# A graph network on one core: layer 0 sums its first 208 edge tiles by counting, and table biases come from TensorE

## Chip, cores and metric

The kernel runs on one core of a Trainium2 chip. The metric is the device time of one execution in microseconds. In the text, PE is TensorE, DVE is VectorE, ACT is ScalarE, POOL is GpSimd and SP is SyncE; PEld is the loading of weights into PE, PEclk the share of its clock that PE was granted, and SPq is the queue from which SP issues transfers.

## The reference

There are 3125 nodes with 128 features, x, and 100,000 edges from `src` to `dst`, sorted by `dst`. Each edge has 16 attributes and one of four types. Two layers follow each other, each with a residual and a layer norm. Cut to what matters:

```python
msgs   = x[src]                                     # layer 0
summed = segment_sum(msgs, dst, n_nodes)
deg    = segment_sum(ones, dst, n_nodes)
h      = layernorm(x + elu((summed / max(deg, 1)) @ W + b))

xl = einsum('nf,rfh->nrh', h, W_l) + b_l            # layer 1, r is one of 4 types
xr = einsum('nf,rfh->nrh', h, W_r) + b_r
z  = leaky_relu(xl[src, type] + xr[dst, type] + edge_features)
# attention of 4 heads: a softmax of z . att over the edges of one node and type,
# weighted sums of xl[src, type], means and gates over types, layer norm, a small MLP, layer norm
```

Layer 0 is a mean over incoming edges of a row of x, a product with W, and a norm. Layer 1 needs, for every node and type, a row of two tables, `xl` and `xr`, with 512 columns each.

## The kernel before

The edges are cut into 784 tiles of 128 (`TT`), in order of `dst`, and four tiles are a quad (`NQ` = 196 quads). The main path is the function `windows`. A second path, `general`, runs afterwards and overwrites the output if a check of the data (the row `bad`, summed into `flag`) says that the quads span more nodes than the main path allows.

**Preparation.** `src`, `dst` and the types are loaded by rows, transposed on PE into columns (`src_e`, `loc_e`, `typ_e`: one column per tile, one partition per edge), and turned into masks. `loc_e` is an edge's node relative to its tile's window. `tmr` is a one-hot over the four types.

**Layer 0's loop.** It has one step per quad. A gather (`gather`) is an indirect transfer issued by POOL: it fetches 128 rows of x by the indices in `src_e` into `xg`, which has 24 buffers. In a step,

- `onehot4` makes on DVE, for each of the four tiles, a one-hot of the edges' local node (`oh`, 32 wide); `sums0` multiplies on PE `oh` by the gathered rows (`sg`, four products of 129 columns, the last column being ones for the degree), and after each product issues the gather of the tile 24 further on. ACT copies the result to `sgs`;
- `spread0` makes on DVE a second one-hot (`ohq`), `out0` multiplies by it on PE (`fo`), and `add0` adds `fo` on DVE into `acc0`, at a column that is read from `d0_i` into a register;
- `masked`, `turned` and `keep` prepare layer 1's edge features: DVE multiplies the quad's attributes by the type's one-hot (`em`), PE transposes (`mp`), ACT copies (`emt`), and SP stores to `eam_d`. The attributes come in seven chunks of 112 rows (`load_chunk`; the last has 109 whole rows), which `turn_chunk` transposes into `ee` (`erows` has one buffer).

**Blocks.** A block is 128 nodes, 25 of them (`NB2`). When the sorted edges have passed a block's nodes (`behind`), `block` puts its work into the following steps: `take`, `mean`, `stats`, `scaled`, `turn` end layer 0 for the block, `lin` makes 16 extra columns, and `table(r)`, one type per step, makes the rows of both tables: on PE the products with `wl` and `wr` (`xp`), on DVE the additions of the bias tables `cl` and `cb`, both held for all 128 partitions (into `xlr` and `xf`), on ACT a rounded copy `xh`. `half(r)` subtracts that on DVE and stores both halves to `xr_d`; a last job stores `xlr` to `xl_d` for all four types at once.

**Order.** The object `Ordered` (its `issue` is L647, so most instructions carry that line) makes each engine issue in program order. `at_step(s, engine, f)` puts a job into a step; the loop at the end of the layer runs the jobs of a step around the fixed parts:

```python
if s < NQ:
    turned(s)
if 0 < s <= NQ:
    keep(s - 1); out0(s - 1)
if s + 1 < NQ:
    onehot4(s + 1); masked(s + 1)
...                                   # jobs for DVE and ACT
if s < NQ:
    spread0(s)
if 0 < s <= NQ:
    add0(s - 1)
if s < NQ:
    sums0(s)
```

Weights for the biases are prepared in the first steps (`linear_weights`, `constant`), and `rows_of_sources` turns `src_e` into indices of `xl_d` (`xli_e`) and the type mask into `tng`.

**Layer 1** begins when the pools of layer 0 are released and its tables are stored. It has again one step per quad: POOL gathers rows of `xl_d`, SP loads windows of `xr_d` (`win`) and the stored attributes (`ea`), PE sums them up in `z`, and so on. After it follow a norm, a small MLP and the output.

Of the kernel before, what the change touches and what calls it, by code (L numbers as in the profile page):

```python
# [624 lines left out]
TC = TT // TR  # L625
GT = 8
# [35 lines left out]

def windows_of(u):
    k = 4 if u < UQ else 2 if u < UP else 1
    return [(i, k) for i in range(0, 4, k)]
# [15 lines left out]
def windows(ctx: ExitStack, tc: tile.TileContext, a, out, flag):  # L681
# [13 lines left out]
    xli_e = S["xli_e"] = cst.tile([P, TT], I32, name="xli_e")  # L695
# [10 lines left out]
    tng = cst.tile([P, TT, R], BF16, name="tng")  # L706
# [35 lines left out]
    with tc.tile_pool(name="l0c", bufs=1) as l0c:  # L742
        acc0 = l0c.tile([P, 2, NPW], F32, name="acc0")
        src_e = l0c.tile([P, TT], I32, name="src_e")

        XG = 24
        xg = l0c.tile([P, XG, F + 1], F32, name="xg")
        nc.vector.memset(xg[:, :, F:], 1.0)
        pool = Ordered(tc, nc.gpsimd)
# [5 lines left out]
        with tc.tile_pool(name="pr", bufs=1) as pr, tc.tile_pool(name="prp", bufs=2, space=PSUM) as prp:  # L755
# [26 lines left out]

            srci = rows("srci", "src", 0, nc.scalar)
# [7 lines left out]
            bad = pr.tile([P, 8], F32, name="bad")  # L791
# [3 lines left out]
            nc.vector.memset(acc0, 0.0)  # L795

            src = floats("src", srci)
            to_e(src_e, src)
            for t in range(XG):
                gather(t)  # L800
# [25 lines left out]
            rF, rL, rB = (rfl[:, i] for i in range(3))  # L826
            wt = prp.tile([TR, TC], F32, name="fp_")
# [9 lines left out]
            nc.vector.tensor_copy(d0_i, rB[0:1])  # L837
            typ = floats("typ", typi)
            to_e(typ_e, typ)
            tm = l0c.tile([P, TT, R], BF16, name="tmr")  # L840
# [29 lines left out]
            rF4, rL4 = (x[0:1].rearrange("p (u i) -> p u i", i=4) for x in (rF, rL))  # L870
            for j, (w, x, y) in enumerate((
# [4 lines left out]
                count(1 + j, n)  # L876

# [7 lines left out]
            bp = prp.tile([1, 8], F32, name="bp", bufs=1)  # L885
# [18 lines left out]
        with tc.tile_pool(name="m0c", bufs=1) as m0c, tc.tile_pool(name="l0", bufs=2) as l0, \  # L904
# [4 lines left out]
            one = l0e.tile([1, 1], F32, name="one")  # L909
            nc.vector.memset(one, 1.0)  # L910
# [12 lines left out]
            fb = l0e.tile([P, TT], F32, name="fb")  # L923
# [4 lines left out]
            cl = m0c.tile([P, R, XW], F32, name="cl")  # L928
            cb = m0c.tile([P, R, HC], F32, name="cb")
# [11 lines left out]
            def load_table_weights():  # L941
# [4 lines left out]
                sp.dma_start(cl[:, :, :HC], bass.AP(tensor=a["L1_gnn_b_l"].tensor, offset=a["L1_gnn_b_l"].offset,  # L946
                                                    ap=[[0, P], [HC, R], [1, HC]]))
# [30 lines left out]
            def rows_of_sources():  # L978

                ve.tensor_scalar_min(xli_e, typ_e, float(R - 1))  # L980
                ve.scalar_tensor_tensor(xli_e, src_e, R, xli_e, op0=OP.mult, op1=OP.add)
                ve.tensor_scalar(tng, tm, 1.0, BIG, op0=OP.subtract, op1=OP.mult)

            def linear_weights(r, w):
                def f():

                    at_ = m0.tile([P, HC], F32, name="xf")
                    sp.dma_start(at_, bcast(a["L1_gnn_att"][r], HC, P))
                    tmp = m0.tile([P, HC], F32, name="tmp", bufs=1)
                    ve.tensor_mul(tmp, w[:, r, :HC], at_)  # L990
                    ve.tensor_reduce(w[:, r, HC:XW], tmp.rearrange("p (h c) -> p h c", h=H), AX.X, OP.add)
                    ve.tensor_scalar(w[:, r, HC:XW], w[:, r, HC:XW], SLOPE, None, op0=OP.mult)
                return f

            def constant(r):
                def f():
# [3 lines left out]
                    cp = bank().rearrange("p a b -> p (a b)")  # L1000
                    pe.matmul(cp, cr[:, r:r + 1].to_broadcast([DR + 1, P]), cw, start=True, stop=True)
                    act.activation(cb[:, r], cp, AF.Copy)
# [3 lines left out]
            for i, f in enumerate([edge_weights, rows_of_sources] +  # L1006
                                  [linear_weights(r, w) for r in range(R) for w in (wl, cl)] +
                                  [constant(r) for r in range(R)]):
                at_step(4 + i, "ve", f)
# [4 lines left out]
            def load_chunk(c):  # L1014
                rows = erows[c] = l0e.tile([TR, P * DE], F32, name="earow")
                v = a["edge_attr_16"].rearrange("e d -> (e d)")
                w = P * DE
                o = c * TR * w
# [667 lines left out]
```

## Time and profile before

| | |
|---|---|
| median of three runs | 3029.38 us (3024.73 to 3030.09) |
| profiled execution, its own time | 3014.4 us |
| its span, first to last instruction | 3012.6 us |
| busy over the span: PE, DVE, ACT, POOL | 84%, 60%, 29%, 52% |
| first gather of x | 20.3 us |
| layer 0's loop, first `sg` product | 64 us |
| last `sgs` copy of layer 0 | 1157.8 us |
| last write of `xh` | 1225.3 us |
| first gather of `xl` (layer 1) | 1234.6 us |
| granted PE clock, mean | 0.851 |

How to read it: the span is the profiled execution; everything in it is in microseconds from its start. The 40 slices of the page are 75.3 us each, and a digit is the busy share of a slice in tenths. A line of an answer on busy time by stage gives the stage, its length, then for each engine the busy time and the number of instructions, the granted PE clock, the share of the transfer engines and GB/s. A line of the timeline gives the start, the duration, the engine, the line of the source, the operation, output and inputs, and in brackets the idle time of the engine before it with what ended it. A line of the waits gives who waited for whom, in total, how often, and the longest.

### The profile page before, as it was taken

To read this page: it belongs to the slowest core of one execution; us is meant where nothing else is said; L and a number is where in the kernel's file an instruction comes from. 1 tells how busy PE (TensorE), PEld (TensorE's weight loads), DVE (VectorE), ACT (ScalarE), POOL (GpSimd) and SP (SyncE) were. 2 spreads that over 40 slices of the span, in tenths; PEclk is the share of its full clock that TensorE was granted. 3 is DMA by queue.
4 is the path that set the end of the run, shared out by engine and by line. 5 is a ranking of instruction groups with operands and counts; after the bars stand their busy time and mean duration, and the time that the engine had idled before them with its cause. 6 is when DMAs were issued, how large, how long until landed. Compare 5 with 4: busy or idle time off the path is not lost.

```text
span 3012.6 us, 69650 instructions
## 1 busy us (share of the span) xinstructions
PE 2521.1 (84%) x25681; PEld 1858.9 (62%) x25681; DVE 1794.3 (60%) x6092; ACT 867.3 (29%) x1872; POOL 1552.6 (52%) x1578
## 2 busy tenths in 40 slices
PE   2867777767567777699999999999999999999952
PEld 1444444434244343477777777888888888788832
DVE  6523445455455565367666667667666666566667
ACT  1212223233233232233333333333333333233211
POOL 5777777777756650444444444444444444444200
PEclk9555667677767687899999999999999999999956
DMA  5433545465445554777777777888888899999710
GB/s 154 141 111 98 162 140 184 162 202 186 154 172 191 174 185 169 271 225 221 221 227 221 222 224 231 256 257 255 255 258 252 255 260 259 245 253 258 189 34 23
DMA packets 278166, 599.24 MB, mean 199 GB/s; under 512 B 47142, under 2 KB 98647, under 8 KB 273820
## 3 DMA queue, kind: packets, MB, share of 16 engines
q1 hardware_dynamic: 186568, 334.42, 34.2%
q0 software_dynamic: 87808, 258.61, 30.5%
q8 instruction: 206, 3.38, 0.5%
q10 hardware_dynamic: 3440, 1.66, 0.3%
q14 instruction: 144, 1.17, 0.1%
HBM read 460.02 MB, written 134.48 MB: 197 GB/s over the span
## 4 chain that ended last, share of the span: by engine, by line
PE 50%; DMA 6%; DVE 3%; issue 0%; SPq 0%; ACT 0%; DVEq 0%; ACTq 0%
PE z L647 30%; PE row L647 9%; PE ag L647 6%; DMA win<-xr_d 4%; PE fo L647 2%; PE sm_p L647 2%; DMA ea<-eam_d 1%; DMA out_dram<-o 0%; DMA fh_all<-fh_d 0%; DMA rm<-rm_d 0%; PE hm L1640 0%; DVE fst L1599 0%; PE xp L647 0%; DMA xr_d<-xh 0%; SPq L647 0%
## 5 line engine op out<-in xcount | busy, mean ns | idle before, releaser
L647 POOL DMA_INDIRECT xl<-xl_d,xli_e x784 | 754.0, 962 | 958.3 <-DVE r L647 326.1
L647 POOL DMA_INDIRECT xg<-in_x_dram,src_e x784 | 797.4, 1017 | 323.0 <-issue 132.0
L647 ACT ACTIVATE relu<-z 128x512 f32<-128x512 f32 x784 | 468.4, 597 | 1104.5 <-PE z L647 1102.7
L647 PE MATMUL z<-f_ident,xl 128*128 128x128 f32 x3136 | 475.6, 274 | 0.0
L647 PEld LDWEIGHTS z<-f_ident,xl 128*128 128x128 f32 x3136 | 368.5, 141 | 44.5 <-issue 0.6
L647 PE MATMUL z<-ea,weh 128*128 128x512 f32 x784 | 383.9, 490 | 12.6 <-DMA sg<-seg_d 12.6
L647 PE MATMUL z<-oht,win 96*128 96x128 f32 (+2 forms) x1600 | 346.9, 298 | 16.5 <-DMA win<-xr_d 16.2
L647 PEld LDWEIGHTS z<-oht,win 128*128 128x128 f32 (+1 forms) x1600 | 276.8, 190 | 77.0 <-DMA win<-xr_d 10.3
L647 PE MATMUL z<-ea,wel 128*128 128x512 f32 x784 | 311.3, 397 | 0.0
L647 PE MATMUL fo<-ohq,sgs 128*128 128x64 f32 x784 | 168.3, 357 | 164.2 <-ACT sgs L647 68.5
L647 PE MATMUL sg<-xg,oh 128*32 128x129 f32 x1568 | 200.6, 361 | 122.8 <-DMA xg<-in_x_dram,src_e 120.7
L647 PEld LDWEIGHTS fo<-ohq,sgs 128*128 128x128 f32 x784 | 153.7, 274 | 193.0 <-ACT sgs L647 130.7
L647 PE MATMUL row<-relu,attw 128*32 128x128 f32 x6272 | 248.5, 276 | 0.0
L647 PEld LDWEIGHTS sg<-xg,oh 128*32 128x32 f32 x1568 | 64.5, 126 | 281.6 <-DMA xg<-in_x_dram,src_e 184.3
L647 DVE TENSOR_TENSOR oh<-loc_e,iw 128x128 f32<-128x128 bf16 (+1 forms) x294 | 99.1, 337 | 217.1 <-PE sg L647 216.7
L647 PE MATMUL ag<-xl,wo 128*32 128x128 f32 x6272 | 218.8, 280 | 3.4 <-DVE wo L647 3.4
L647 PEld LDWEIGHTS z<-ea,weh 128*128 128x128 f32 x784 | 148.1, 189 | 89.6 <-issue 89.5
L647 PE MATMUL mp<-f_ident,em 128*128 128x128 f32 x784 | 178.8, 369 | 11.0 <-issue 5.1
L647 ACT ACTIVATE xh<-xf 128x512 fp32r<-128x512 f32 x100 | 63.0, 630 | 431.5 <-DVE xf L647 257.1
L647 PEld LDWEIGHTS row<-relu,attw 128*32 128x32 f32 x6272 | 164.0, 110 | 32.7 <-issue 32.7
L647 PEld LDWEIGHTS ag<-xl,wo 128*32 128x32 f32 x6272 | 164.4, 112 | 7.2 <-DVE wo L647 3.7
L647 DVE TENSOR_TENSOR acc<-acc,fo 128x128 f32 (+1 forms) x392 | 99.5, 254 | 115.0 <-issue 44.1
(270 smaller groups left out, 3602.4 us busy)
## 6 DMA issues: line engine op xcount, KB each, us to landing
win<-xr_d SPq DMA_DIRECT2D x224, 256.0 KB
xr_d<-xh SPq DMA_DIRECT2D x100, 512.0 KB
eam_d<-emt SPq DMA_DIRECT2D x196, 256.0 KB
ea<-eam_d SPq DMA_DIRECT2D x196, 256.0 KB
win<-xr_d SPq DMA_DIRECT2D x176, 192.0 KB
xl_d<-xlr SPq DMA_DIRECT2D x25, 1032.0 KB
sg<-seg_d SPq DMA_DIRECT2D x196, 128.0 KB
rm<-rm_d SPq DMA_DIRECT2D x392, 32.1 KB
```

The lines of the kernel that those rows point to most:

```text
L647: ins = f(*args, **kw)
```

## The change

**Counting.** The first 52 quads (`UD`; 208 tiles, `TD`), whose nodes are below 240 (`ND`), no longer gather. For a tile, DVE makes two one-hots in bf16: `ol`, 128 wide, of the source node's low seven bits, and `oc`, 200 or 300 wide, of its upper bits times 8 or 12 plus the local destination. PE multiplies them (`cn`, in a PSUM tile called `dn`), summed over the quad's four tiles: how often each source occurs at each destination. `count_add` adds this on DVE to `A`, 128 x 25 x 252. At the end `counted_sums` multiplies on PE, for each of 25 source blocks, the block of x and a matrix of ones by `A` (240 columns), and one addition puts the sums and degrees into `acc0`.

**The loop** has 144 steps (`NS`), from quad 52 on. 52 counts are spread over its first 39 steps or so, counted sums over the following 13. `turned_by` spreads all 196 quads of edge attributes over 140 steps. Edge attributes come in 14 chunks of 56 rows, the last with 53 whole rows. Blocks 0 and 1 come after the counted sums, the others 52 steps earlier than before. The jobs of a step stand in another order, with the copy `sgs` first on ACT.

**Biases.** `cl` and `cb` go. One small tile, `cbl` (four partitions, in fp32r, the biases as high and low halves), is multiplied by two rows of ones (`two`) on PE, ahead of each table product into the same PSUM tile. ACT copies the sums out (`xh`, `xlr`), DVE only makes the low half. `xl_d` is stored one type at a time, two steps after its table.

**Buffers.** `src_e` and `tm` are overwritten in place by what was `xli_e` and `tng`, in `rows_of_sources`, which moves from the start to step `NS`. `fb` lies in `wl` until that is loaded. `xh` and `xlr` have three buffers, `xp` three instead of four, `em` four, `oh` three. Three checks are added to `bad`.

The diff, cut to its core:

```diff
+UD, ND, SHI = 52, 240, NB2
+def counted(u):
+    return 8 if u < 24 else 12
...
-            for t in range(XG):
+            for t in range(TD, TD + XG):
                 gather(t)
...
+            nc.vector.tensor_scalar_min(dc_i, rF4[:, :UD, 0], float(ND - 1))
...
+            for u0, u1, j in ((0, 24, 8), (24, UD, 9)):
+                nc.vector.scalar_tensor_tensor(sj[:, :u1 - u0], rF4[:, u0:u1, 0], float(counted(u0) - 1),
+                                               rL4[:, u0:u1, 3], op0=OP.add, op1=OP.is_lt)
+                count(j, u1 - u0)
+            nc.vector.tensor_scalar(bad[0:1, 10:11], rL[0:1, TD - 1:TD], float(ND - 1), None, op0=OP.is_gt)
...
-            cl = m0c.tile([P, R, XW], F32, name="cl")
-            cb = m0c.tile([P, R, HC], F32, name="cb")
+            cbl = m0c.tile([4, R, XW], F32R, name="cbl")
+            two = m0c.tile([4, 2, P], F32R, name="two")
...
             def rows_of_sources():
-                ve.tensor_scalar_min(xli_e, typ_e, float(R - 1))
-                ve.scalar_tensor_tensor(xli_e, src_e, R, xli_e, op0=OP.mult, op1=OP.add)
                 ve.tensor_scalar(tng, tm, 1.0, BIG, op0=OP.subtract, op1=OP.mult)
+                ve.tensor_scalar_min(typ_e, typ_e, float(R - 1))
+                ve.scalar_tensor_tensor(src_e, src_e, R, typ_e, op0=OP.mult, op1=OP.add)
+            def halves(r, p0, row):
+                n = row.shape[-1]
+                hi = m0.tile([1, 2, XW], F32R, name="xh", bufs=3)
+                act.activation(hi[:, 0, :n], row, AF.Copy)
+                ve.tensor_sub(hi[:, 1, :n], row, hi[:, 0, :n].bitcast(F32))
+                for i in range(2):
+                    sp.dma_start(cbl[p0 + i:p0 + i + 1, r, :n].bitcast(F32), hi[:, i, :n].bitcast(F32))
...
+            def turned_by(s):
+                return min(NQ, (s + 1) * NQ // (NS - 4) + 1)
...
+            def count_columns():
+                ve.memset(A, 0.0)
+                ve.tensor_scalar(tmp_i, src_e[:, :TD], P - 1, None, op0=OP.bitwise_and)
+                ve.tensor_copy(lo_f, tmp_i)
+                ve.tensor_scalar(tmp_i, src_e[:, :TD], 7, None, op0=OP.logical_shift_right)
+                ve.tensor_copy(c_f, tmp_i)
+                for u0, u1 in ((0, 24), (24, UD)):
+                    c = c_f[:, 4 * u0:4 * u1]
+                    ve.tensor_scalar(c, c, float(counted(u0)), -200.0, op0=OP.mult, op1=OP.add)
+                ve.tensor_add(c_f, c_f, loc_e[:, :TD])
+            def count(u):
+                w = counted(u)
+                cn = l0p.tile([P, SHI, w], F32, name="dn")
+                for i in range(4):
+                    t = 4 * u + i
+                    ol = l0.tile([P, P], BF16, name="ol", bufs=4)
+                    ve.tensor_scalar(ol, il, lo_f[:, t:t + 1], None, op0=OP.is_equal)
+                    oc = l0.tile([P, SHI * w], BF16, name="oc", bufs=4)
+                    ve.tensor_scalar(oc, ic[:, :SHI * w], c_f[:, t:t + 1], None, op0=OP.is_equal)
+                    pe.matmul(cn.rearrange("p a b -> p (a b)"), ol, oc, start=(i == 0), stop=(i == 3))
+                X["cn", u] = cn
+            def count_add(u):
+                n = nc.values_load(dc_i[0:1, u:u + 1], engines=[ENG.DVE], min_val=0, max_val=ND - 1, ...)
+                v = A[:, :, ds(n, counted(u))]
+                ve.tensor_tensor(v, v, X.pop(("cn", u)), op=OP.add)
...
+            def counted_sums(k):
+                if k == 0:
+                    X["dn"] = l0p.tile([P, 2, ND], F32, name="dn")
+                for i, w in enumerate((X.pop(("xc", k)), ones)):
+                    pe.matmul(X["dn"][:, i], w, A[:, k, :ND], start=(k == 0 and i == 0), stop=(k == SHI - 1 and i == 1),
+                              skip_group_check=True)
+                if k == SHI - 1:
+                    ve.tensor_tensor(acc0[:, :, :ND], acc0[:, :, :ND], X.pop("dn"), op=OP.add)
+            C0 = 3
+            for u in range(UD):
+                at_step(C0 + u * 3 // 4, "count", u)
+            C1 = C0 + (UD - 1) * 3 // 4 + 2
+            for k in range(SHI):
+                at_step(C1 + k // 2 - 1, "sp", lambda k=k: x_load(k))
+                at_step(C1 + k // 2, "ve", lambda k=k: counted_sums(k))
+            C2 = C1 + SHI // 2 + 1
...
                 def table(r):
-                    xp = m0p.tile([P, HC], F32, name="xp", bufs=4)
-                    pe.matmul(xp, d["ht"], wl[:, r, :HC], start=True, stop=True)
-                    xq = m0p.tile([P, HC], F32, name="xp", bufs=4)
-                    pe.matmul(xq, d["ht"], wr[:, r], start=True, stop=True)
-                    ve.tensor_add(d["xlr"][:, r, :HC], xp, cl[:, r, :HC])
-                    d["xf", r] = m0.tile([P, HC], F32, name="xf")
-                    ve.tensor_add(d["xf", r], xq, cb[:, r])
-                    d["xh", r] = m0.tile([P, 2, HC], F32R, name="xh")
-                    act.activation(d["xh", r][:, 0], d["xf", r], AF.Copy)
+                    xp, xq = (m0p.tile([P, HC], F32, name="xp", bufs=3) for _ in range(2))
+                    xa = m0p.tile([P, H], F32, name="mw")
+                    for o, w, i, c in ((xq, wr[:, r], 1, cbl[:, r, :HC]), (xp, wl[:, r, :HC], 0, cbl[:, r, :HC]),
+                                       (xa, wl[:, r, HC:], 0, cbl[:, r, HC:])):
+                        pe.matmul(o, two[:, i], c, start=True, stop=False)
+                        pe.matmul(o, d["ht"], w, start=False, stop=True)
+                    xl = d["xl", r] = m0.tile([P, XW], F32, name="xlr", bufs=3)
+                    xh = d["xh", r] = m0.tile([P, 2, HC], F32R, name="xh", bufs=3)
+                    act.activation(xh[:, 0], xq, AF.Copy)
+                    act.activation(xl[:, :HC], xp, AF.Copy)
+                    act.activation(xl[:, HC:], xa, AF.Copy)
...
+                def store(r):
+                    sp.dma_start(xl_v[b][:, r], d["xl", r])
+                    sp.dma_start(xr_v[b][:, r], d["xh", r].bitcast(F32).rearrange("p s w -> p (s w)"))
...
-                block(b, behind(b) + 1)
+                block(b, max(behind(b) - UD, C2 + 4 * b if b * P < ND else 0) + 1)
...
             for s in range(last + 1):
+                u = UD + s
...
+                if UD < u <= NQ:
+                    out_copy(u - 1)
+                new = list(range(done, turned_by(s))) if s < NS else []
+                for v in new:
+                    turned(v)
+                if UD < u <= NQ:
+                    out0(u - 1)
+                counts = jobs.pop((s, "count"), [])
+                if counts:
+                    count(counts[0])
+                if u + 1 < NQ:
+                    onehot4(u + 1)
...
+                for i, v in enumerate(counts):
+                    count_add(v)
+                    if i + 1 < len(counts):
+                        count(counts[i + 1])
+                if UD < u <= NQ:
+                    add0(u - 1)
...
+                if u < NQ:
+                    spread0(u)
+                    sums0(u)
+                for v in new:
+                    keep(v)
```

## The prediction

> **What bounds the kernel now.** I read the 40 slices first, then busy time by stage, then the waits of each stage. The chain of waits is lost before 1182 us (records are missing there), so it says nothing of layer 0. In the slices POOL, the engine that issues the gathers of x, is busiest in the first two fifths while PEclk is low; later PE is at 9 and PEclk at 9.
>
> ```profile
> PE   2867777767567777699999999999999999999952
> POOL 5777777777756650444444444444444444444200
> PEclk9555667677767687899999999999999999999956
> ```
>
> Layer 0's loop runs 196 steps (4 tiles each) from 64 to 1158 us; layer 1's first gather starts at 1234.6. By the ends of the steps' `sgs` copies I cut this into stages: steps 0 to 143, a stop, seven quick steps (4.8 us each), 44 slow steps, the tail.
>
> ```profile
> core 0: us, PE busy (x) PEld busy (x) DVE busy (x) ACT busy (x) POOL busy (x), PEclk, DMA share, GB/s
> 248.00:799.00 551.00, 417.04 (x2050) 250.98 (x2049) 268.86 (x724) 155.54 (x323) 422.40 (x423) 0.68 0.51 166
> 799.00:837.00 38.00, 3.42 (x21) 1.77 (x21) 5.32 (x15) 3.00 (x6) 18.30 (x20) 0.59 0.31 100
> 871.00:1158.00 287.00, 212.82 (x983) 116.95 (x983) 157.13 (x417) 87.30 (x176) 160.86 (x158) 0.75 0.52 180
> ```
>
> From 248 to 799 POOL issues 423 gathers in 551 us, one in 1.30 us: 0.94 us of work, 0.30 us of issue, some lengthening. Four make 5.2 us, and a step takes (799 - 64)/144 = 5.1 us. **So 144 steps are bound by the gathers.** From 871 on a step takes 6.5 us and POOL is idle almost half of the time. The waits say why, first for 150 to 740 us, then for 870 to 1130 us (total us, times, longest):
>
> ```profile
> PEld sg L647 <- DMA xg<-in_x_dram,src_e: 169.5, 135, 4.2
> PE sg L647 <- DMA xg<-in_x_dram,src_e: 114.1, 107, 3.7
> ```
> ```profile
> POOL xg L647 <- PE sg L647: 48.9, 27, 3.8
> PE fo L647 <- ACT sgs L647: 32.9, 17, 2.5
> PE fo L647 <- DVE acc L647: 27.7, 22, 2.1
> ```
>
> First PE waits for gathered rows; later POOL waits for PE, which is slowed by the tables of one block in every five steps or so and waits for ACT and DVE before `fo`. The stop is a third limit:
>
> ```profile
> 793.65 14.10 SPq L647 DMA_DIRECT2D xr_d<-xh  x1
> ```
> ```profile
> 834.57 0.63 ACT L647 ACTIVATE xh<-xf 128x512 fp32r<-128x512 f32 x1 [34.95 <-DMA xr_d<-xh]
> ```
>
> **What the Trainium skill says.**
> (1) "SBUF — State Buffer", section "Who interferes with whom": a VectorE instruction in a 2-port mode, or with two SBUF inputs, and GpSimd lock each other out. The trace agrees: a gather that starts inside such an instruction is lengthened to about its end.
>
> ```profile
> 32.84 3.42 DVE L841 TENSOR_TENSOR tmr<-typ_e,ir 128x3136 bf16<-128x3136 bf16 x1
> 33.22 3.87 POOL L647 DMA_INDIRECT xg<-in_x_dram,src_e  x1 [0.30 <-issue]
> ```
>
> (2) "VectorE: DVE Perf Modes", section "The perf-mode tier table": bf16 `tensor_scalar` in SBUF reaches four elements a cycle. The trace's `tng<-tmr` agrees: 3136 elements in 0.97 us. None of this size with a per-partition operand is shown.
> (3) "TensorE: Matmul & The Clock Gate", section "What's actually happening": TensorE's clock is halved until it has been busy for some microseconds. It agrees: 0.68 here, 1.00 in layer 1.
> (4) "DMA: Bandwidth & Descriptors", section "Why a DMA increments its semaphore by 16 and not by 1": the number of DMA engines divides the partition count, 127 go to one engine. The stop is this: the last edge chunk loads 109 rows (a prime) of 8 KB at 793.1 us, and stores of `xh` queue behind it until 834.6.
>
> **The change, part by part.** Steps fall from 196 to 144, starting at tile 208. I sum layer 0 to the first gather of layer 1.
>
> Start. Before, the loop starts at 64 us. New ahead of it on DVE: zeroing A (6300 elements, 5.3 us at the rate of the 6528-element memset, 5.50), zeroing cbl (some 1.8), six operations on 208 columns (some 2), a second masked product (0.7) and small copies; the smaller first chunk takes some 1 less. Loop at **73 us**. The first 24 gathers are issued earlier, so nothing hides these 9.
>
> Steps 0 to 43, with counting. Removed for good are 208 gathers: 208 x 1.30 = 270 us of POOL. Remaining gathers take 5.2 us a step. DVE: 52 counts in 39 steps, 1.33 a step, each 4 x (`ol` 128 + `oc` 200 or 300, bf16). `ohq`, with a pointer operand, takes 0.27 us for 64 f32; so an `ol` or `oc` costs 0.2 to 0.3 if four elements a cycle hold, 0.35 to 0.5 if one. I take 0.22 at the pitch: 8 x 0.22 + 0.5 for adding to A (`acc` 0.29 at 128 wide, up to 300 here, and a register load) = 2.3 a count, 3.0 a step. Beside this: `em` 0.62 x 1.36 (196 masked products over 140 steps), `oh` 0.21, `acc` 0.3, `ohq` 0.2, chunk 0.15, three blocks 0.4: 2.1. DVE **5.1 us a step** (6.7 at the dear end), just under POOL. But they exclude each other: for 3.6 us of a step (one-hots 2.4, `em`, `oh` and `ohq` 1.2) DVE holds what gathers need, and a gather then waits 0.1 us (rest of one one-hot) to 0.85 (half a run of eight). Times four gathers: 0.2 to 1.4. I take 5.2 + 0.6 = **5.8, 44 steps, 255 us** (5.3 to 6.7). PE's counting matmuls, 5.3 a step at about 0.15 to 0.3 us, lie beside the gathers. Weight preparation now sends 16 small `cbl` stores through SP, with `eam_d` stores behind them; four `emt` buffers cover that, and without them each row costs some 3 us.
>
> Steps 44 to 143. PE work in a step at full clock, from the timeline near 1057 us: transposes of `em` 0.43, `sg` 0.36, `fo` 0.46, tables 0.92 + 0.95 for one r; with `lin` and the smaller products 3.4 us a step in the slow stage. Busy 213 of 287 us, 4.8 a step: an effective clock of 0.7. After: 1.36 times the transposes (+0.15), two 512-column and one 4-column fp32r bias matmuls for each r (nearest row `z<-ea,wel`, pitch 0.23; 0.46 at half clock): +0.5, so 4.0 us. The 200 adds of `cl` and `cb` (0.69 us each, 138 us of DVE) go; ACT gets 100 copies of 512 (0.60) and 100 of 4 (0.2), some 80 us, reaching about 3 us a step: hidden. What is late next is PE: 4.0/0.75 = 5.3 beside 5.2 for gathers. The waits before `fo` were (32.9 + 27.7)/40 = 1.5 us a step; `sgs` is now copied first on ACT and DVE has fewer adds, so I keep 0.5. **5.8, 100 steps, 580 us** (5.25, gathers alone, to 6.9, PE at 0.7 with the old waits). The 50 matmuls of `counted_sums` (240 columns, some 0.4 to 0.8 us each) over 13 steps are in that bound.
>
> Stop. The last chunk has 53 rows, again a prime: 53/109 of 34 to 38 us = **16 us**.
>
> Tail. Before 1158 to 1235, 77 us. `rows_of_sources` moves here from step 5: 0.97 + 0.56 + 0.98 = 2.5 us of DVE, offset by the missing adds. The tables leave in 100 stores of 258 KB beside the 100 of `xr_d` instead of 25 of 1032 KB: 75 more issues of 0.4 us on SP, which waits anyway. **77 us** (70 to 85).
>
> Sum: 73 + 255 + 580 + 16 + 77 = 1001, against 1235: **234 us less**. Layer 1 is the same instructions on the same tables: nothing. The profiled execution takes 3014.4 (span 3012.6, 1.8 around it): 2780. The median of the three runs is 15.0 above the profiled one: 3029.4 - 234 = **2795 us**.
>
> **Rivals.**
> A, gathers bind throughout: 73 + 144 x 5.25 + 16 + 77 = 922, 313 less, 2716. For it: PE with shorter waits keeps its clock up. Against: PE at 0.68 clock in the gather-bound stage.
> B, PE becomes the bound: 6.3 and 6.9 us a step, tail 85: 73 + 277 + 690 + 16 + 85 = 1141, 94 less, 2935. For it: PE's larger work at the old clock. Against: the seven steps after the stop, with gathers ready, took 4.8 us each.
> C, slower: DVE's one-hots and POOL's gathers take turns on the shared port. If an `ol` or `oc` cost 0.55 us at the pitch, DVE would hold the port 10.7 x 0.55 + 1.2 = 7.1 us a step, and 5.2 us of gathers would add to it: 12.3 x 44 = 541 instead of 255, +286, 3081. It decides from 11.1 us a step, (255 + 234)/44. Against: the long gather above got in as soon as `tmr` ended.
> D, the new span checks send the kernel to `general`, milliseconds more: a quad's span there is 2 x 3125 x u/196/196 nodes, 3.9 at u = 24 against 8 and 8.5 at 52 against 12; practically excluded.
>
> **How the numbers follow.** Forecast (2740 to 2865) 0.6, A 0.17, B 0.17, C and D 0.05, no visible difference 0.01. A measurement of this kernel tells about 0.2% (6 us). The range 2705 to 2900 takes A, the forecast and the near side of B: 0.8. Faster 0.94, same 0.01, slower 0.05.
>
> **What would show it.** 576 `xg` gathers; `sgs` copies 5.8 us apart in both stretches; `ol` and `oc` near 0.25 us; `xg` lengthened in the counting steps; a stop near 16 us; layer 1's first `xl` gather near 1000 us. Gathers near 5.25 a step say A; POOL waiting for PE all along says B; `xg` means of 2 us while counting say C. If layer 1 changes its length, the premise is wrong.

## The result, and the profile after

The changed kernel is **slower**: 3148.87 us, median of four runs (3141.7 to 3158.41), against 3028.76 us for the kernel before beside it; the ratio is 1.0401, with a 95% interval of 1.0371 to 1.0431. The prediction was 2795 us (2705 to 2900). The profiled execution took 3158.41 us, with a span of 3156.5 us. Three sets of the experiments below (group 2, the end of group 4, group 5) ran on chips on which every kernel is slower, with 3259 to 3305 us for the kernel before, so they are set against the kernel before on the same chip.

The 40 slices of the changed kernel's page, now 78.9 us each, are read first, as before:

```profile
PE   1578899999999899989999999999999999999952
POOL 4475464255444341044444444444444444434200
PEclk9555595555555555569999999999999999999956
```

PE reads 9 from the sixth slice on (8 in two slices), as a bound engine does, and POOL has fallen from 7 to 4 or 5 in most slices. But PEclk stands at 5 nearly all through layer 0, the first and the sixth slice apart. Before, it moved between 5 and 9: the records of its clock have 108 stretches, against 22 now, and from 481.6 to 1389 us the changed kernel has one single stretch, at half clock. PE was busy, and stayed at half clock. (The records of all runs here hold only two clocks, 1 and 0.5.) Busy time by stage of the changed kernel (columns as in the prediction: stage, its length, then busy time and instructions of each engine, clock, share of the transfer engines, GB/s), cut at the end of the counting steps, at the last `sgs` copy and at the first `xl` gather:

```profile
core 0: us, PE busy (x) PEld busy (x) DVE busy (x) ACT busy (x) POOL busy (x), PEclk, DMA share, GB/s
73.00:391.00 318.00, 244.38 (x1136) 143.47 (x1135) 201.26 (x769) 78.35 (x168) 175.04 (x172) 0.54 0.39 119
391.00:1260.00 869.00, 803.87 (x2761) 430.26 (x2759) 268.16 (x799) 284.59 (x592) 378.10 (x381) 0.55 0.44 147
1260.00:1373.00 113.00, 105.83 (x160) 41.17 (x160) 24.53 (x83) 28.04 (x61) 0.29 (x1) 0.50 0.32 121
1373.00:3150.00 1777.00, 1666.21 (x21672) 1356.04 (x21672) 1181.06 (x4450) 550.86 (x1223) 753.69 (x784) 0.96 0.77 224
```

The last line stops 6.5 us before the end of the span; layer 1 to the end took 1784 us, against 1778 before, a difference smaller than that between runs of one kernel. Layer 0 is 138 us longer than before (1373 against 1235) and 372 us longer than predicted (1001). In the 100 steps of the second line PE is busy 8.0 us of 8.7 at a clock of 0.55. The waits of the changed kernel from 540 to 1030 us (who waited for whom, total us, times, longest):

```profile
POOL xg L648 <- PE sg L648: 219.0, 48, 11.8
DVE acc L648 <- PE fo L648: 205.8, 45, 6.4
PEld xp L648 <- issue: 102.1, 131, 1.5
```

POOL and DVE wait for PE. The third line is the odd one: the weight loads for the tables (bias matmuls and products) stood idle 102 us, up to 1.5 us at a time, for nothing that the profile shows. The timeline has the place. One table (one type of one block) in the changed kernel, PE alone, start and duration first:

```profile
893.50 0.79 PE L648 MATMUL xp<-cbl,two 4*128 4x512 f32 x1
894.22 2.08 PE L648 MATMUL xp<-wr,ht 128*128 128x512 f32 x2
896.22 0.79 PE L648 MATMUL xp<-cbl,two 4*128 4x512 f32 x1
896.94 2.08 PE L648 MATMUL xp<-wl,ht 128*128 128x512 f32 x2
898.95 0.37 PE L648 MATMUL mw<-cbl,two 4*128 4x4 f32 x1
899.25 0.59 PE L648 MATMUL mw<-wl,ht 128*128 128x4 f32 x2
899.77 0.64 PE L648 MATMUL sg<-xg,oh 128*32 128x129 f32 x6
```

From 893.50 to 899.77 is 6.27 us. The four-row bias matmuls (`4*128`) start 0.72 us ahead of the product that follows, and each product of two passes holds PE for 2.00 us, although two passes of such a product, unbroken, start 0.85 us apart at half clock in the kernel before. Yet the lines look like gapless work.

The other readings that answer to those of before: the third limit, the last edge chunk, is there with 12.7 us, and the gathers are hardly lengthened by the one-hots: 1020 ns in the mean in the counting steps, 994 in the 100 steps after them (waits from 1030 to 1090 us, then groups of instructions of the whole execution: busy us, mean ns, idle time before them).

```profile
PE mp L648 <- DMA earow<-in_edge_attr_dram: 12.7, 1, 12.7
```
```profile
L648 POOL DMA_INDIRECT xg<-in_x_dram,src_e x576 | 586.8, 1019 | 625.3 <-PE sg L648 465.6 <-issue 102.0 <-PE mp L648 17.2
L648 DVE TENSOR_SCALAR ol<-il,lo_f 128x128 bf16<-128x128 bf16 x208 | 53.1, 256 | 0.0
L648 DVE TENSOR_SCALAR oc<-ic,c_f 128x300 bf16<-128x300 bf16 x112 | 35.2, 318 | 0.0
```

### The profile page after: what moved, and what is told of

The parts are those of the page before. It is cut to its first block, busy times and chain, and to the rows that moved or that the text cites. A ratio compares the mean times of both kernels' runs of the same rounds, so it can differ in the third digit from the quotient of the medians.

```text
span 3156.5 us, 69765 instructions
## 1 busy us (share of the span) xinstructions
PE 2830.8 (90%) x25777; PEld 1978.7 (63%) x25777; DVE 1730.8 (55%) x6238; ACT 945.2 (30%) x2050; POOL 1342.4 (43%) x1371
## 4 chain that ended last, share of the span: by engine, by line
PE 79%; DMA 8%; DVE 7%; ACT 2%; issue 1%; SPq 0%; DVEq 0%; ACTq 0%
PE z L648 28%; PE xp L648 17%; PE row L648 8%; PE mp L648 6%; PE ag L648 6%; PE fo L648 5%; PE mw L648 4%; DMA win<-xr_d 3%; PE dn L648 2%; PE sg L648 2%; DMA sg<-seg_d 2%; PE sm_p L648 1%; DMA earow<-in_edge_attr_dram 1%; ACT emt L648 1%; DVE oc L648 1%
## 5 line engine op out<-in xcount | busy, mean ns | idle before, releaser
L648 POOL DMA_INDIRECT xl<-xl_d,src_e x784 | 754.0, 962 | 1008.7 <-DVE r L648 304.5
L648 POOL DMA_INDIRECT xg<-in_x_dram,src_e x576 | 586.8, 1019 | 625.3 <-PE sg L648 465.6
L648 DVE TENSOR_TENSOR acc<-acc,fo 128x64 f32 (+1 forms) x340 | 84.7, 249 | 431.0 <-PE fo L648 364.7
L648 PE MATMUL mp<-f_ident,em 128*128 128x128 f32 x784 | 206.6, 415 | 71.7 <-ACT emt L648 41.4
L648 PEld LDWEIGHTS mp<-f_ident,em 128*128 128x128 f32 x784 | 132.7, 207 | 145.2 <-ACT emt L648 63.0
L648 PE MATMUL xp<-wl,ht 128*128 128x512 f32 x200 | 200.9, 1107 | 0.0
L648 PE MATMUL xp<-wr,ht 128*128 128x512 f32 x200 | 200.9, 1107 | 0.0
L648 ACT ACTIVATE emt<-mp 128x512 fp32r<-128x512 f32 x196 | 117.0, 597 | 162.7 <-PE mp L648 160.7
L648 PEld LDWEIGHTS xp<-cbl,two 4*128 4x128 f32 x200 | 55.2, 276 | 158.8 <-issue 142.2
L648 DVE TENSOR_TENSOR xh<-xp,xh 128x512 fp32r<-128x512 f32 x100 | 68.7, 689 | 156.2 <-ACT xh L648 155.9
```

What stands on the lines that cost most here:

```text
L648: ins = f(*args, **kw)
```

## The experiments

**The theories.** After reading the two traces I held that the few rows of the bias matmuls keep PE's clock at half, since the clock would follow the share of the array at work (T1). The rivals: the unbroken run of products is what the clock needs, and the bias matmuls cut it up (T2); counting, or the greater work of a step, holds the clock down (T3).

### Group 1: is it the bias matmuls, and what about them?

Without the bias matmuls (the tables then lack their bias terms):

```diff
-                        pe.matmul(o, two[:, i], c, start=True, stop=False)
-                        pe.matmul(o, d["ht"], w, start=False, stop=True)
+                        pe.matmul(o, d["ht"], w, start=True, stop=True)
```


> The changed kernel without its 300 bias matmuls (the tables' bias terms are left out). Layer 0 took 1373 us to the first xl gather with them. T1 (four-row matmuls between the products keep TensorE's granted clock at half): the clock switches up again as before, mean near 0.85, layer 0 some 250 to 370 us shorter, so 2780 to 2900. T3 (counting, or the greater work of a step, holds the clock down): the clock stays at 0.5 to about 1300 us; only the matmuls' own time goes, 200 x 0.72 + 100 x 0.1 = 150 us at half clock, so about 3000.

With 128 rows:

```diff
-            cbl = m0c.tile([4, R, XW], F32R, name="cbl")
-            two = m0c.tile([4, 2, P], F32R, name="two")
+            cbl = m0c.tile([P, R, XW], F32R, name="cbl")
+            two = m0c.tile([P, 2, P], F32R, name="two")
```


> The changed kernel with the same bias matmuls on 128 rows instead of 4 (124 rows of zeros; same columns, same results). T1 (few rows are what holds the clock down, because the clock follows the array's activity and not the busy time): clock up again, mean above 0.84, total 2800 to 2950. T2 (breaking up the dense run of products is what counts, whatever the rows) and T3 (counting and the greater work): as the changed kernel, within 20 us of 3150, clock at 0.5 to about 1390 us.

With four rows, grouped:

```diff
-                    for o, w, i, c in ((xq, ...), (xp, ...), (xa, ...)):
+                    three = ((xq, ...), (xp, ...), (xa, ...))
+                    for o, w, i, c in three:
                         pe.matmul(o, two[:, i], c, start=True, stop=False)
+                    for o, w, i, c in three:
                         pe.matmul(o, d["ht"], w, start=False, stop=True)
```


> The changed kernel with the three bias matmuls of a table first and its three products with ht back to back after them. T2 (the run of products was broken up): clock up again, mean above 0.84, 2800 to 2950. T1 (four-row matmuls) and T3 (greater work): within 30 us of 3150, clock at 0.5 to about 1390 us.

The kernel before with the biases by TensorE, and no counting:

```diff
-                    ve.tensor_add(d["xlr"][:, r, :HC], xp, cl[:, r, :HC])
-                    ve.tensor_add(d["xf", r], xq, cb[:, r])
...
+                        pe.matmul(o, two[:, i], c, start=True, stop=False)
+                        pe.matmul(o, d["ht"], w, start=False, stop=True)
...
+                    act.activation(d["xlr"][:, r, :HC], xp, AF.Copy)
```


> The kernel before with nothing but the biases moved to TensorE: 196 steps, all 784 gathers, no counting; 300 bias matmuls as in the change, copies on ACT in place of the adds on DVE. T1 and T2: the clock stays at 0.5 for long stretches of layer 0, the slow steps go from 6.5 to about 9 us, total 3100 to 3300. T3 (counting holds the clock down): clock as before, 0.85, total 3000 to 3060.

One run each, beside 3019.83 us for the kernel before:

| kernel | us | to before | clock, 250 to 900 us |
|---|---|---|---|
| no bias matmuls | 2731.05 | 0.904 | 0.83 |
| bias matmuls of 128 rows | 2765.58 | 0.916 | 0.85 |
| four rows, grouped | 2828.62 | 0.937 | 0.80 |
| before, biases by TensorE, four rows | 3206.47 | 1.062 | 0.56 |

In the same stretch the kernel before has 0.68 and the change 0.57. The clock by slices, in this order:

```profile
PEclk9996687898879799999999999999999999999856
```
```profile
PEclk9999688888978989999999999999999999999956
```
```profile
PEclk9997698878877879999999999999999999999956
```
```profile
PEclk9555555665555555559999999999999999999956
```

The nines at the left end of the first three rows are not to be trusted. In these three traces the records of the clock begin only between 194.7 and 249.4 us, and what lies before them counts as full clock. The transposes of `em` show that it was not: in the kernel with 128 rows, four of them take 1.12 us just before the first record, as in later stretches recorded at half clock, and 0.66 just after it.

```profile
245.33 1.12 PE L648 MATMUL mp<-f_ident,em 128*128 128x128 f32 x4
251.53 0.66 PE L648 MATMUL mp<-f_ident,em 128*128 128x128 f32 x4
```

The first table of this kernel starts at about 250 us, so the half clock before it has nothing to do with the bias matmuls.

Three things follow. The loss is the four-row matmuls': added alone to the kernel before they cost 6.2%, with nothing counted, so T3 falls. It is not their number or their columns: with 128 rows, 124 of them zeros, the same 300 matmuls leave the kernel 383 us faster than the change. And it is not the four rows alone: grouped, they bring the clock back nearly as well. T1 had put the grouped kernel near 3150, T2 the padded one; both came in under 2830, so neither theory stands alone. (The first two runs also came in under the ranges expected of T1, 2780 to 2900 and 2800 to 2950 us.)

What the padded kernel does in layer 0, by stage, for comparison with the changed one (same columns; `xl` starts at 981.5 us; the clock of the first line counts 73 to 249 us as full and is about 0.59 if that part was at half, an estimate from the transposes above):

```profile
73.00:356.00 283.00, 210.38 (x1150) 135.46 (x1147) 201.65 (x768) 78.06 (x170) 181.41 (x174) 0.90 0.43 135
356.00:928.00 572.00, 473.68 (x2743) 314.59 (x2741) 266.13 (x798) 274.61 (x591) 377.37 (x379) 0.87 0.67 223
928.00:981.50 53.50, 45.42 (x160) 26.66 (x160) 24.24 (x83) 25.75 (x61) 0.00 (x1) 0.95 0.66 255
```

### Group 2: the other half alone, and the number of rows

The four kernels: 32 rows and 64 rows (the same edit as for 128); the kernel before with biases on 128 rows; and the change without its bias matmuls, with the biases added by DVE (from tables kept in bf16), called counting alone:

```diff
-                        pe.matmul(o, two[:, i], c, start=True, stop=False)
-                        pe.matmul(o, d["ht"], w, start=False, stop=True)
...
-                    act.activation(xl[:, :HC], xp, AF.Copy)
+                    ve.tensor_add(xl[:, :HC], xp, cl[:, r, :HC])
+                    ve.tensor_add(d["xf", r], xq, cb[:, r])
```


> The counting half of the change alone: sources counted for the first 208 tiles, biases added by DVE as in the kernel before (kept as bf16, so that they fit; the adds of 512 are 0.69 us each in the kernel before), no bias matmul. Against the kernel without bias terms (2731 us), 300 adds on DVE in place of 200 copies on ACT, some 1.4 us a step where DVE is busy 2.1 to 3.1 of 5 us. If the loss is the bias matmuls' alone: 2720 to 2800, about 230 to 300 under the kernel before, which makes counting the whole gain. If the adds hold up PE's buffers again: 2850 to 2900.

> The kernel before with only the biases moved to TensorE (3206 us with four rows), on 128 rows instead. T1 (few rows hold the clock down, counting has no part in it): the clock comes back, 2960 to 3060, as the kernel before, since gathers bind 144 of its steps. If the loss in that kernel came from the matmuls' time or from the copies on ACT: 3180 to 3220.

> As the kernel with bias matmuls of 128 rows (2765.6 us), but 32 rows: 4 used, 28 of zeros. If the clock follows the number of rows at work in a window of 3.4 us: a table of one r at half clock has 1.8 us of bias matmuls to 4.5 us of products, so a window's mean share of rows is 0.72 with 4 rows, 0.78 with 32, 0.86 with 64, 1 with 128; 32 rows then lie near 4 rows: 2950 to 3150, clock at half for most of the tables. If any row group of 32 counts as a whole array or only very small matmuls are discounted: 2760 to 2830.

> The same with 64 rows. If the share of rows at work in a window counts (0.86 here): between the two ends, 2780 to 2950, and faster than with 32 rows. If all 128 rows are needed (a change of the row count itself is what stops the clock): 3100 to 3170, as with 4 rows. If row groups of 32 count as a whole: 2760 to 2790.

On this chip the kernel before took 3305.43 us. Counting alone: 3041.9 us, 0.920. Biases on 128 rows alone: 3293.42 us, 0.996. 32 rows: 3340.57 us, 1.011. 64 rows: 3232.67 us, 0.978. Against 3020 us these ratios would be 2779, 3009, 3052 and 2953 us, as estimates: ratios are not quite the same on the two kinds of chip (128 rows with the split chunk, below: 0.907 and 0.924). By these the first three met what was expected of their likeliest cases (32 rows that of T1), and 64 rows lay a little above the top of T1's range; group 3 has 64 rows on a chip of the faster kind. **Counting is the whole gain**, 8% without the biases on TensorE; "counting" here includes what else the change does to loop, chunks and buffers, which was not taken apart. The biases on TensorE bring nothing to be seen in one run without it, even in the better form. DVE's 300 adds, which the change took away, seem to have been hidden: with them the kernel is no slower, by ratio, than with padded bias matmuls on such a chip (0.924, the control of group 5), and its first `xl` gather starts at 1152 us against 1145. The time falls as rows are added, which looked like T1.

### Group 3: four, 64 and 128 rows on one chip, and a version to beat both

In the padded kernel PE stood still once for long. The timeline of that kernel, the transposes of the last edge chunk:

```profile
812.52 0.66 PE L648 MATMUL mp<-f_ident,earow 56*128 56x56 f32 x4 [19.58 <-DMA earow<-in_edge_attr_dram]
```

The edit that splits the chunk's 53 rows into 48 and 5 goes into all four kernels:

```diff
-                sp.dma_start(rows[:full], v[o:o + full * w].rearrange("(p x) -> p x", x=w))
+                f0 = full if full == ER else full // 16 * 16
+                sp.dma_start(rows[:f0], v[o:o + f0 * w].rearrange("(p x) -> p x", x=w))
+                if f0 < full:
+                    sp.dma_start(rows[f0:full], v[o + f0 * w:o + full * w].rearrange("(p x) -> p x", x=w))
```


> A version meant to beat both: bias matmuls on 128 rows, and the last edge chunk's 53 rows loaded as 48 and 5. In the kernel with 128 rows alone (2765.6 us, 0.916 of the kernel before) PE stands still for 19.6 us behind that load, which moves 25 GB/s for some 20 us. If one queue's rate on a prime count of rows is the cause: the gap goes, 17 to 20 us less, 0.910 of the kernel before. If the load was late for another reason (its issue, the stores ahead of it): the gap stays, 0.915 to 0.917.

> The same with the three bias matmuls of a table first and its products back to back. If a window's share of rows is all that counts, the order is nothing once all have 128 rows: within 8 us of the kernel with the split alone. If back-to-back products by themselves help the clock: 15 to 40 us less.

> The changed kernel (four rows) with the last chunk split: row count 4 on the same chip as the others, split the same. Share-of-rows theory: clock at half for most of the tables, 1.03 to 1.04 of the kernel before, some 12 us under the changed kernel.

> The same with 64 rows. Share-of-rows theory: a window holding a whole bias matmul has a share of 0.87 to 0.89 and rises in part of the cases, so between 4 and 128 rows: 0.94 to 1.0 of the kernel before. If groups of 32 rows count as whole, within 10 us of 128 rows; if only all 128 count, within 10 us of 4 rows.

| kernel, chunk split | us | to before (3025.59) |
|---|---|---|
| 128 rows | 2746.0 (5 runs) | 0.9071, 0.9051 to 0.9091 |
| 128 rows, grouped | 2763.09 (5 runs) | 0.9136, 0.9116 to 0.9156 |
| 64 rows | 3018.65 | 0.998 |
| four rows | 3135.42 | 1.036 |

The 128-row kernel with the split chunk beats both: 9.3% under the kernel before. The wait for the chunk is gone, and the eight steps around it took 46.8 us instead of 64.1: 17.3 us. Grouping with 128 rows was expected to do nothing or to help; it costs 17 us, for a reason that I did not find. Four rows with the split are 13 us under the change, as expected. 64 rows lie between, at the upper end of T1's range.

### Group 4: share of rows, or a pause at the change?

Looking at whole tables in these traces showed something else (below): the table takes the same time with 4, 32 and 64 rows, and much less with 128. So PE may pause at each change between few rows and 128. Kernels with 120 and 96 rows were to tell the two theories apart, by the same edit.

> Bias matmuls of 120 rows (chunk split as in the kernel of 2746.0 us). If a window's share of rows decides (0.98 in a window with a whole bias matmul): the clock rises as with 128 rows, 0.907 to 0.915 of the kernel before. If the pause at a change of row count decides: as with 64 rows or worse, 0.99 to 1.04, with a bias matmul at half clock still 0.72 us to the next start.

> The same with 96 rows. Share of rows (0.95 in a window with a whole bias matmul, 0.94 to 0.97 over its places): between 64 rows (0.998) and 128 (0.907), near the latter: 0.91 to 0.95. Pause at a change of row count: 0.99 to 1.04.

120 rows: 2751.91 us, 0.9105 of 3022.56. 96 rows: 2761.24 us, 0.9135. Both as T1 expected; but the pause had gone from both as well, so the runs could not decide. Between 64 rows and 96 two things change. 68 rows keep the share of 64:

> Bias matmuls of 68 rows. If the pause between matmuls of at most 64 rows and of 128 is what matters: bias matmul and product 1.5 us from start to start at half clock, and the time with 96 rows, 0.910 to 0.920 of the kernel before. If the share of rows streamed matters by itself: near 64 rows, 0.97 to 1.0. If the pause comes with any count under some value between 68 and 96: 2.73 us, and 0.98 to 1.0, which leaves both open.

> 32 rows, pause as with 4 and 64. If only the pause matters, the number of rows below 64 is nothing: near 4 and 64 rows, which themselves differ (1.036 and 0.998). If rows count as well: between the two, 1.005 to 1.03.

On a chip where the kernel before took 3258.58 us, 68 rows gave 3010.23 us, **0.924**, and 32 rows 3303.47 us, 1.014. For 128 rows on such a chip there is 0.9239 (the control of group 5). Four more rows of zeros are worth as much as 64 more. The length of layer 0 says the same: on the slower chips the first `xl` gather starts at 1344 us with 64 rows (chunk not split), at 1135 with 68 and at 1145 with 128. T1 falls as I had put it: the main step is not in the share of the rows, but in which side of 64 they lie. The 32 rows came in as expected if rows count as well (1.005 to 1.03), but four rows were not run on such a chip. The weight loads show the pause. The same group of instructions (busy us, mean ns, then the idle time before them) in the changed kernel, with 64 rows, with 68 rows, and with 128:

```profile
L648 PEld LDWEIGHTS xp<-cbl,two 4*128 4x128 f32 x200 | 55.2, 276 | 158.8 <-issue 142.2 <-DVE ohq L648 3.0 <-DVE em L648 3.0
```
```profile
L648 PEld LDWEIGHTS xp<-cbl,two 64*128 64x128 f32 x200 | 50.7, 254 | 134.8 <-issue 122.6 <-DVE ohq L648 2.3 <-DVE ee L648 1.5
```
```profile
L648 PEld LDWEIGHTS xp<-cbl,two 68*128 68x128 f32 x200 | 48.0, 240 | 36.8 <-issue 31.3 <-ACT xlr L648 1.9 <-DVE me L648 0.5
```
```profile
L648 PEld LDWEIGHTS xp<-cbl,two 128*128 128x128 f32 x200 | 42.9, 214 | 31.2 <-issue 24.3 <-ACT xlr L648 2.7 <-DVE acc L648 1.5
```

With 4 and 64 rows the load of the bias matmul's weights waits 0.6 to 0.7 us each time for nothing that the profile shows; from 68 on it waits 0.12 to 0.16. "TensorEngine Tiling (Array Packing)" of the Trainium skill, section "Tiling Modes", offers a cause: tilings of 64 and of 32 rows are modes of their own, and a change of mode drains TensorE. The edge between 64 and 68 rows and these waits agree with it. That a plain matmul of at most 64 rows is put into such a mode by itself is argued from them; no run shows the mode. In whole tables, from the start of the first bias matmul to the start of the next other matmul, medians in us over the tables that have one recorded clock throughout and no other table right behind them. The last column has, of all 100 tables of a kernel, those that lie wholly at half clock:

| bias matmuls | at full clock | at half clock | tables at half clock, of 100 |
|---|---|---|---|
| none | 1.98 | 3.88 | 10 |
| 128 rows | 2.60 | 4.99 | 4 |
| 96 rows, 120 rows | 2.60, 2.61 | 4.98, 4.99 | 6 and 6 |
| 68 rows | 2.61 | 4.99 | 8 |
| four rows, grouped | 2.70 | 5.08 | 10 |
| 64 rows | 3.48 | 6.27 | 47 |
| 32 rows | 3.47 | 6.27 | 92 |
| four rows (the change) | 3.47 | 6.27 | 93 |

The pauses cost 0.87 us a table at full clock and 1.28 at half (four rows against 128). And where they are, the clock is at half for many more of the tables (47 to 93 of 100 against 4 to 10), which costs more: 3.47 to 6.27. "TensorE: Matmul & The Clock Gate" (section "What's actually happening") says that the clock rises after a window of about 3.4 us in which PE was busy. The records of the granted clock agree in one point: the times between its changes are multiples of 3.41 us. Inside a table, six pauses leave no such window without one, two pauses (grouped) leave a run of products of 3.7 us at half clock (four passes of 0.85 us and the small products). That the pauses themselves count as idle in the window is argued from this, not measured. Nor do they bring the clock down every time: seven tables of the changed kernel ran at full clock, between 393 and 482 us.

One thing stays open. 4 and 64 rows have the same table times and yet 1.036 and 0.998 on one chip, with 90 and 47 of 100 tables at half clock (both with the split chunk). So the number of rows, or something that goes with it, has a part in the clock after all, beside the pause.

### Group 5: are there such pauses elsewhere in the change?

The smaller edge chunks are transposed with 56 rows where the kernel before had 112, and each block's mean has a matmul of one row. Both were put on 128:

```diff
-                    pe.transpose(tp[:, k], rv_[:, k0 + k], ident[:ER, :ER])
+                    pe.transpose(tpf[:, k], rv_[:, k0 + k], ident)
...
-                    pe.matmul(mw[:, F:], d["me"][0:1, 1], ones[0:1, 0:1], start=True, stop=True)
+                    pe.matmul(mw[:, F:], d["me"][:, 1], ident[:, 0:1], start=True, stop=True)
```


> The kernel with bias matmuls of 128 rows and the split chunk (2746.0 us, 0.907), and in addition the transposes of the edge chunks on 128 rows (72 of zeros) and the mean's matmul of one row on 128. Start of a 56-row transpose after fo at full clock: 0.35 us where the kernel before, with 112 rows, had 0.11. If that pause is paid at every change: 56 runs of four transposes and 25 means, some 160 changes of 0.1 to 0.25 us, 15 to 40 us less than the control, partly hidden by waits. If these places are hidden beside gathers or waits: within 5 us of the control.

> The control: the kernel with bias matmuls of 128 rows and the split chunk, once more, on the chip of the run beside it: 0.905 to 0.909 of the kernel before.

On a chip with 3285.05 us for the kernel before: 3028.3 us, 0.921 (0.9189 to 0.9232), the control 3034.7 us, 0.9239 (0.9212 to 0.9266), on this chip not the 0.905 to 0.909 that was expected of it. The intervals overlap; no gain is shown. The distance from `fo` to the first of these transposes at full clock, 0.35 us in the median of the control, stayed at 0.35 us with 128 rows, so it was no change of row mode, and the premise of this run was wrong.

## Why the prediction was wrong, point by point

**The step that failed** is the one for steps 44 to 143: "What is late next is PE: 4.0/0.75 = 5.3 beside 5.2 for gathers." The 4.0 us of PE work at full clock were nearly right: 8.0 us busy at 0.55 are 4.4, and in the padded kernel 4.7 at 0.87 are 4.1. The 0.75 was wrong. I took the clock as a number that the kernel before had (0.68 to 0.75) and that would stay near it; rival B, with 0.7, did the same. It is an outcome of how PE's work is laid out, its lower end in these records is 0.5, and nothing in my range had that case. With 0.55 the same step gives 4.0/0.55 + 0.5 = 7.8 us; measured were 8.7, with the stop (0.13 a step). What is left is of the size of the pauses, which the sum did not have at all.

**The price of the bias matmuls** was taken from `z<-ea,wel`, a matmul of 128 rows: 0.5 us a step at full clock. With 128 rows that was near (2.60 - 1.98 = 0.62). With four rows it is 3.47 - 1.98 = 1.49 us at full clock and 6.27 - 3.88 = 2.39 at half. The nearest row of the trace had the right columns and type, but not the right number of rows.

**By stages**, predicted, measured, and measured with 128 rows:

| | predicted | the change | 128 rows |
|---|---|---|---|
| loop starts | 73 | 72.9 | 72.4 |
| steps 0 to 43 | 255 | 318 | 283 |
| steps 44 to 143, with the stop | 596 | 869 | 572 |
| tail | 77 | 113 | 53.5 |
| first `xl` gather | 1001 | 1372.7 | 981.5 |

With 128 rows, and so without the pauses, the sum stands within 20 us, and the kernel at 2765.58 us within the range. Some of that is luck: the counting steps are 28 us over, the next 100 and the tail 24 and 24 us under. Still, the reasoning on gathers, DVE and the queues was near, with these sizes off. The counting steps of the padded kernel took 6.4 us in the mean instead of 5.8: the first 16, beside the preparation of weights, 7.4, and the other 28 the 5.8 of the forecast. What held up the first 16 was not tried; PE was at half clock there, before any table. An `ol` or `oc` was priced too high: they follow each other at 0.16 to 0.21 us instead of 0.22 (0.26 to 0.32 from start to end). The stop was 12.7 us in the changed kernel, 19.6 in the padded one, 17.3 when taken away; its sum in the prediction, 53/109 of 34 to 38, is 16.5 to 18.5 and not 16. The tail was too long by 24 us, probably since I had left its PE work at the old clock.

**The rivals.** Rival B had the sign of the waits right (POOL waited 465.6 us for `sg`, all along) and the clock too high. Rival C ended on the side that came true, for a reason that was false: `xg` took 1019 ns in the mean, 1017 before, and 1020 in the counting steps, so one-hots and gathers did not take turns. Layer 1 was "nothing", and that held within 6 us.

**What I had read past.** PEld in the page of before is the row that could have warned: it overlaps PE there, and I never asked what a four-row load does to that overlap.

## What to carry to other kernels

A small matmul put between large ones on TensorE is priced by its row count as well as its columns: here, bias matmuls of 4, 32 or 64 rows between products of 128 cost 0.87 us a table in pauses at full clock, and often the clock as well. Padding with rows of zeros past 64, or doing the small ones in one run, takes that away. A PE that reads 9 in tenths at a PEclk of 5 is not a PE at its limit: look at the idle time before its weight loads ("issue"). Price a step's PE work at half clock for the slow end of a range. And check a clock that is read from a page against the times of one kind of matmul: the records may begin late.

## What the runs showed of the hardware that I had not expected

- With 68 rows a table took 4.99 us at half clock, with 64 rows 6.27: an edge between two sizes that do almost the same work.
- Rows of zeros are not free of effect: 124 of them made the kernel 383 us faster.
- TensorE stayed at half clock for 908 us while the profile showed it busy nearly all the time (803.87 of 869 us from 391 to 1260); the busy times of matmuls hide the pauses.
- A load of 53 rows of 8 KB held PE up for 12.7 to 19.6 us; as 48 and 5 rows it was not seen.
- Single chips differ: the kernel before took 3020 to 3029 us on some and 3259 to 3305 us on others. Layer 1, with the same code, took 1778 to 1790 us in the traces of the former and 1873 to 1897 in those of the latter, and the padded kernel with the split chunk reached layer 1 at 959 us and at 1145. Its ratio to the kernel before was 0.907 on the former, 0.924 on the latter.
